# Context layers of 16 heads: second-half maxima moved into the batch's own attention, maxima spread among projections, shift chain apart

## The chip, the core and the metric

The kernel runs on one NeuronCore of a Trainium2 chip. A core has a matrix engine (TensorE, PE in the profile, with its weight loads listed apart as PEld), a vector engine (DVE), an activation engine (ACT), a general engine (POOL) and a queue that issues transfers (SP). [...] The metric is the device time of one execution in microseconds (us), lower is better.

## The reference, cut to what matters

The program is a chain of attention layers over `x` of 4 batches, 1024 tokens and 256 channels. The context `ctx` has 77 tokens a batch. Everything is float32.

```python
# layer "sa"+"ca": pre-norm self-attention (16 heads, masked), cross-attention to ctx (16 heads of 16), feed-forward 256 -> 1024 -> 256
h = layernorm(x, ln1);  x = x + mha(h, h, h, sa, mask)
h = layernorm(x, ln2);  x = x + mha(h, ctx, ctx, ca)
h = layernorm(x, ln3);  x = x + relu(h @ w1 + b1) @ w2 + b2
# three layers of 4 heads of 64: the first attends to ctx, two to themselves
for i in range(3): x = layer4(x, ctx if i == 0 else x)
# "l2" and "l3": cross-attention to ctx, 16 heads of 16, residual, post-norm ("l2" has an output projection)
for layer in (l2, l3):
    scores = einsum(q, k) / scale          # per batch: 16 x 1024 x 77
    attn = softmax(scores)
    x = layernorm(attn @ v [@ wo] + x)
return x
```

The softmax subtracts each row's maximum before the exponential. In this kernel that maximum is found by computing the scores a first time with tokens on the partitions ("maxima"), and is then added into the scores of the attention proper, which have keys on the partitions, by a small matmul ("shift").

## The kernel before

**Items and units.** `Net.rest` lines up 28 items: layers `sa` (class `SelfFew`), `ca` (`Cross16`), three layers of 4 heads (`Cross4`, then `Self4` twice), `l2` and `l3` (`Cross16` both), each for batches 0 to 3. In this text "l2 1" is layer l2 on batch 1. `Pipe.run` goes through the items one after the other. An item's attention is a row of units; a `Cross16` item has 8: four groups of four heads (g = 0..3) for the first half of the tokens (c = 0), then four for the second half (c = 1). TensorE's program order is exactly the order in which the Python code emits (`manual_schedule`); the order on the other engines is left to a scheduler, which can put a ready instruction ahead of one emitted earlier.

**One unit** (`Pipe.unit`) emits the scores of a group (line 346, eight matmul records, and line 352, the four matmuls that add the shift), then calls the pump, then emits the finishing transposes of the group before (line 377), and last the weighted sum (line 365) of its own group, which waits for the two exponentials on ACT (line 356).

**The pump** (class `Pump`) puts other work into the units. It has two lists of steps, each with a cost, perhaps a test that must hold and a lag that should pass after it. The first list holds the steps of the next item's `start` (and, for `Self4`, `more` of the item itself); the second holds the steps of the item before's `end`. At unit n of N it takes steps until the done share of all costs reaches n/N, choosing, among list heads whose test holds and whose lag is over, the one of the list that is less far; the last unit takes all that is left, lags or not. If no head is due, the unit ends early. `Pump.until` takes steps of the first list until a test holds: attention on half c asks that `c + 1` halves are prepared.

**The steps of `Cross16.start`** prepare an item while the item before it attends: `new` (tiles; POOL computes the spread keys `ka`; DVE the statistics where a norm comes first), and for each half `norm`, two `turn`s (transposes to channels, line 252), two `query` projections (line 260), eight `maxima` (line 270: two pairs of matmul records each, into two of the four one-bank PSUM tiles `p1`; line 275: two reductions on DVE), `shift`, `have_half`. `shift` first splits the maxima into three bfloat16 parts by four short DVE instructions (lines 304 to 307) and then transposes them on TensorE (line 310) and copies them out, alternately on DVE and ACT (`evac`).

**The steps of `end`** finish the item before: `turn` and `project` (lines 412 and 419; not in l3, which has `plain`), `stats` (lines 1483, 1484) and `norm` (lines 1530, 1533) for l2 and l3, with a reciprocal root on POOL between them; for `ca` the feed-forward (`Feed.steps`, lines 562 to 600), whose matmuls are 16 `hidden` and 8 `out` steps. The normalized tile `xn` (tag "F") has one buffer, shared by `Cross16`, `SelfFew` and `Feed`.

Of the kernel before, what the change touches and what calls it, by code (L numbers as in the profile page):

```python
# [17 lines left out]
P = 128  # L18
# [65 lines left out]
class Pump:  # L84
# [31 lines left out]

    def until(self, test):
        while not test():
            self.take(0)


class Pipe:
# [26 lines left out]
    def run(self, items):  # L149
        pump = Pump(self, 1, items[0].start(), [])  # L150
        pump.until(lambda: items[0].halves >= 1)
        left = pump.lists[0]
        before = None
        for a, b in zip(items, items[1:]):
            b.prev = a
        for i, item in enumerate(items):
            last = i + 1 == len(items)
            first = left + ([] if last else items[i + 1].start())
            second = (before.end() if before else []) + (item.end() if last else [])
            left = []  # L160
            idle = item.idle()
            self.pump = pump = Pump(self, item.units + idle, item.more() + first, second)
            for _ in range(idle):
                self.unit()
            for scores in item.attend():
                self.unit(scores, item.cost)
            before = item
        while self.due:
            pump.n = 0
            self.unit()  # L170
        pump.n = pump.units - 1
        pump()


class Item:
# [4 lines left out]

    def more(self):

        return []

    def idle(self):

# [2 lines left out]
    def __init__(self, net, layer, b):  # L189
        self.net, self.l, self.b = net, layer, b  # L190
        self.halves, self.ended = 0, 0
        self.prev, self.later_half = None, True

    def room(self):

# [9 lines left out]
class Cross16(Item):  # L205
# [7 lines left out]
    def start(self):  # L213

        net, l, b, h = self.net, self.l, self.b, H16
        nc, work, x = net.nc, net.work, net.x[b]
        steps = l.steps() if b == 0 else Steps()
        step = steps.add

        def new():  # L220
            self.hT = net.tile("C", [P, NC, S], name="hT")
            self.sh = net.tile("SH", [P, 2, 512], BF16, name="SH")
            self.mx = net.small.tile([P, NT, h.n], F32, tag="mx", name="mx", bufs=2)
            self.ka = net.work.tile([P, 2, 4, SC], F32, tag="KA", name="KA", bufs=2)
            for e in range(2):
                nc.gpsimd.tensor_tensor(
                    self.ka[:, e, :, :], l.kt[:, e, ts(b, SC)].unsqueeze(1).to_broadcast([P, 4, SC]),
                    net.own4.unsqueeze(2).to_broadcast([P, 4, SC]), ALU.mult,
                )
            if l.norm is not None:  # L230
                self.mv = net.moments(b)
                self.rstd = net.rsqrt_var(self.mv, 1e-5)

        def new_q():
            self.qt = net.tile("A", [P, 2, S], name="QT")

        def norm(c):
            if l.norm is None:
                self.xn = x[:, 4 * c : 4 * c + 4, :]
                return  # L240
            mv, rstd = self.mv, self.rstd
            self.xn = net.tile("F", [P, 4, C], name="xn")
            for i in range(4):
                t = 4 * c + i
                nc.vector.tensor_scalar(
                    self.xn[:, i, :], x[:, t, :], mv[:, t, 0:1], rstd[:, t : t + 1], ALU.subtract, ALU.mult
                )

        def turn(c, cc):
            pt = net.p1.tile([P, 512], F32, tag="p1", name="pt")  # L250
            for i in range(4):
                nc.tensor.transpose(pt[:, ts(i, P)], self.xn[:, i, ts(cc, P)], net.ident)
            at = None if l.norm is None else COL_LN + 4 * (l.norm - 1) + cc
            g, be = (None, None) if at is None else (net.cols[:, at : at + 1], net.cols[:, at + 2 : at + 3])
            net.evac(self.hT[:, cc, ts(c, 512)], pt, g, be)

        def query(e, c):
            pp = net.p1.tile([P, 512], F32, tag="p1", name="pp")
            for cc in range(NC):
                nc.tensor.matmul(  # L260
                    pp, l.w["wq"][:, cc, ts(e, P)], self.hT[:, cc, ts(c, 512)], start=cc == 0, stop=cc == NC - 1
                )
            nc.scalar.activation(self.qt[:, e, ts(c, 512)], pp, AF.Identity, bias=net.bias16[:, l.at + e : l.at + e + 1])

        def maxima(e, t):

            pas = [net.p1.tile([P, 4, SC], F32, tag="p1", name="pa") for _ in range(2)]
            for i in range(2):
                rows = slice(64 * i, 64 * i + 64)
                nc.tensor.matmul(  # L270
                    pas[i], self.qt[rows, e, ts(t, P)], self.ka[rows, e, :, :], start=True, stop=True
                )
            for i in range(2):
                out = self.mx[:, t, :].rearrange("p (j g) -> p j g", j=4)[:, 2 * i : 2 * i + 2, 2 * e : 2 * e + 2]
                nc.vector.tensor_reduce(  # L275
                    out, pas[i].rearrange("p (j s) k -> p j s k", s=2), AX.X, ALU.max, negate=True
                )

        ln = l.norm is not None
        step(0, new, lag=8 * ln)  # L280
        for c in range(2):
            step(0, norm, c, lag=3 * ln)
            step(0.5, turn, c, 0)
            step(0.5, turn, c, 1, lag=2)
            if c == 0:
                step(0, new_q, test=self.room)
            for e in range(2):
                step(1.8, query, e, c)
            for e in range(2):
                for i in range(4):  # L290
                    step(0.55, maxima, e, 4 * c + i, lag=3 if (e, i) == (1, 3) else 0)
            step(0.3, self.shift, c)
            step(0, self.have_half)
        return steps

    def shift(self, c):

        net, h = self.net, H16
        nc = net.nc
        m = self.mx[:, 4 * c : 4 * c + 4, :].rearrange("p t (j g) -> p t j g", j=4)  # L300
        m3, rest = net.m3[c], net.rest16[c]
        parts = [m3.rearrange("p t (j r) -> p t j r", j=4)[:, :, :, i : 3 * G : 3] for i in range(3)]
        left = rest.rearrange("p t (j g) -> p t j g", j=4)
        nc.vector.tensor_copy(parts[0], m)
        nc.vector.tensor_tensor(left, m, parts[0], ALU.subtract)
        nc.vector.tensor_copy(parts[1], left)
        nc.vector.tensor_tensor(parts[2], left, parts[1], ALU.subtract)
        pm = net.p1.tile([P, 512], BF16, tag="p1", name="pm")
        for i in range(4):
            nc.tensor.transpose(pm[:, ts(i, P)], m3[:, i, :], net.identb)  # L310
        net.evac(self.sh[:, c, :], pm)

    def shift_by_row(self, c):
# [217 lines left out]
class Feed:  # L531
# [15 lines left out]
    def steps(self, b):  # L547
        net, nc, x = self.net, self.net.nc, self.net.x[b]
        s = {}
        steps = Steps()  # L550
# [6 lines left out]

        def norm(c):
            s["xn"] = net.tile("F", [P, 4, C], name="xn")
            for i in range(4):  # L560
                t = 4 * c + i
                nc.vector.tensor_scalar(
# [3 lines left out]
        def turn(c, cc):  # L566
# [2 lines left out]
                nc.tensor.transpose(pt[:, ts(i, P)], s["xn"][:, i, ts(cc, P)], net.ident)  # L569
            at = COL_LN + 8 + cc  # L570
            net.evac(s["hT"][:, cc, ts(c, 512)], pt, net.cols[:, at : at + 1], net.cols[:, at + 2 : at + 3])

        def hidden(q, f):

# [28 lines left out]
            step(0, self.load)  # L603
        step(0, new, lag=8)
        for c in range(2):
            step(0, norm, c, lag=3)
            step(0.5, turn, c, 0)
            step(0.5, turn, c, 1, lag=2 * c)
        for q in range(4):
# [24 lines left out]
class Self16(Cross16):  # L634
# [8 lines left out]
    def start(self):  # L643
# [18 lines left out]

        def norm(c):
            self.xn = net.tile("F", [P, 4, C], name="xn")
            net.normal(self.xn, x, self.mv, self.rstd, c)

        def turn(c, cc):
            net.turn_normal(self.hT, self.xn, 1, c, cc)

        def query(g, c):  # L670
            pp = net.p1.tile([P, 512], F32, tag="p1", name="pp")
# [49 lines left out]
        step(0, new, lag=8 if b else 0)  # L721
        for c in self.cs:
            if b:
                step(0, norm, c, lag=3)
                step(0.5, turn, c, 0)
                step(0.5, turn, c, 1, lag=2)
            step(1.8, query, 0, c)
# [100 lines left out]
class SelfFew(Cross16):  # L828
# [5 lines left out]
    def start(self):  # L834
# [21 lines left out]

        def norm(c):
            self.xn = net.tile("F", [P, 4, C], name="xn")
            net.normal(self.xn, x, self.mv, self.rstd, c)

        def turn(c, cc):
            net.turn_normal(self.hT, self.xn, 1, c, cc)

        def query(e, c):
            pp = net.p1.tile([P, 512], F32, tag="p1", name="pp")
# [57 lines left out]
        step(0, new, lag=8 if b else 0)  # L923
        for c in self.cs:
            if b:
                step(0, norm, c, lag=3)
                step(0.5, turn, c, 0)
                step(0.5, turn, c, 1, lag=2)
            if c == 1:
# [3 lines left out]
            if c == 1:  # L933
                step(0.9, values)
            for t in range(4 * c, 4 * c + 4):
                step(0.9, maxima, t, lag=3 if t % 4 == 3 else 0)
            step(0.3, self.shift, c)
            step(0, self.have_half)
        return steps
# [495 lines left out]
class Net:  # L1435
    def __init__(self, ctx, tc, t):
        self.ctx, self.tc, self.nc, self.t = ctx, tc, tc.nc, t
        self.flip = 0

    def evac(self, out, src, scale=None, bias=None):

# [694 lines left out]
```

## Time and profile before

| | |
|---|---|
| time, median of 3 runs (lowest to highest) | 2431.14 us (2427.19 to 2433.52) |
| the profiled execution's own time | 2428.16 us |
| its span, first to last instruction | 2426.3 us |
| TensorE busy, matmul / weight load | 91% / 51% of the span |
| VectorE, ScalarE, GpSimd busy | 67%, 37%, 4% |
| mean granted TensorE clock | 0.944 |
| maxima: line 270 matmul / line 275 reductions | 768 records, 170.9 us / 384 reductions, 157.6 us |
| plain 16-head context units: line 346 / line 356 | 112.7 us / 185.4 us |

How to read what follows: the windows view lists, for a stretch given in us from the span's start, each engine's busy time, then the TensorE clock that was granted (1.00 is full speed), then the transfers' share. The timeline lists groups of like instructions: start, length, engine, line, operation, destination and sources, count, and in brackets the idle time of that engine just before and what ended it.

### The profile page before, as it was taken

The page shows a single profiled execution, that of the slowest core. Times are in us where ns is not written, and L with a number is a line of the kernel's source. Part 1 is how long each engine was busy: PE and PEld are TensorE (multiplying, and loading weights), DVE is VectorE, ACT ScalarE, POOL GpSimd, SP SyncE. Part 2 cuts the span into 40 slices and gives each one's busy share as a digit, 9 for nine tenths or more (in the row PEclk, how much of TensorE's full clock was granted, in tenths as well). Part 3 has the DMA queues.
Part 4 walks back from the last instruction along what each step waited for, and adds up shares of the span by engine and source line. Part 5 has one row for each costly group of instructions (what it writes and reads, how often), then busy time and mean ns, then how long its engine had stood idle before and what let it go on. Part 6 is the DMA issues. An engine that isn't in the chain of part 4 may idle for free. (4 is left out here: it accounts for less than half of the span.)

```text
span 2426.3 us, 29759 instructions
## 1 busy us (share of the span) xinstructions
PE 2201.2 (91%) x11003; PEld 1233.3 (51%) x11003; DVE 1620.2 (67%) x3200; ACT 907.2 (37%) x1700; POOL 104.2 (4%) x142
## 2 busy tenths in 40 slices
PE   4899999999999989999998999999998898899886
PEld 2566546666768655544444544444444444454332
DVE  5566655444243777888888788888888655565665
ACT  1222342222331544444444445444433343334333
POOL 2000000000000000000000000000000000000000
PEclk7999999999989989999999999989999898899888
DMA  4000010000000001766665666666675300000000
GB/s 127 18 1 16 5 35 1 1 7 5 7 5 3 1 5 45 157 150 139 139 144 134 146 148 148 139 139 139 156 160 130 70 5 1 5 1 1 27 18 28
DMA packets 197593, 158.18 MB, mean 65 GB/s; under 512 B 51327, under 2 KB 196030, under 8 KB 197438
## 3 DMA queue, kind: packets, MB, share of 16 engines
q1 hardware_dynamic: 195374, 152.45, 27.3%
q0 software_dynamic: 1008, 2.68, 0.5%
q8 instruction: 90, 1.47, 0.3%
q10 hardware_dynamic: 1056, 1.05, 0.1%
q14 instruction: 65, 0.53, 0.1%
HBM read 17.67 MB, written 4.19 MB: 9 GB/s over the span
## 5 line engine op out<-in xcount | busy, mean ns | idle before, releaser
L1230 ACT ACTIVATE PR<-ss,nm 128x1024 f32<-128x1024 f32 x256 | 284.4, 1113 | 398.9 <-DVE nm L1224 313.1
L1242 DVE STREAM_TRANSPOSE PR<-PR 128x2048 f32<-128x2048 f32 x128 | 295.8, 2311 | 113.4 <-ACT PR L1230 109.9
L1213 PE MATMUL ss<-QK 64*128 64x512 f32 x1024 | 336.9, 650 | 38.1 <-ACT PR L1230 37.8
L1224 DVE TENSOR_REDUCE nm<-ss 128x1 f32<-128x1024 f32 x256 | 299.8, 1210 | 9.5 <-PE ss L1213 9.4
L1285 PE MATMUL po<-PT,V 128*64 128x256 f32 x2048 | 261.3, 399 | 9.0 <-DMA PT<-PR 6.8
L356 ACT ACTIVATE PT<-pb 77x1024 f32<-77x1024 f32 x192 | 185.4, 1016 | 173.7 <-PE pb L352 173.7
L1285 PEld LDWEIGHTS po<-PT,V 128*64 128x64 f32 x2048 | 141.7, 141 | 171.6 <-issue 109.2
L1213 PEld LDWEIGHTS ss<-QK 64*128 64x128 f32 x1024 | 116.7, 193 | 181.9 <-ACT PR L1230 105.7
L275 DVE TENSOR_REDUCE mx<-pa 128x4 f32<-128x308 f32 x384 | 157.6, 469 | 74.2 <-PE pa L270 73.1
L270 PE MATMUL pa<-KA,QT 64*128 64x308 f32 x768 | 170.9, 499 | 33.7 <-DVE mx L275 31.1
L270 PEld LDWEIGHTS pa<-KA,QT 64*128 64x128 f32 x768 | 103.4, 201 | 101.9 <-DVE mx L275 46.8
L365 PE MATMUL po<-PT,Vc 77*32 77x512 f32 x768 | 135.7, 646 | 18.9 <-ACT PT L356 10.2
L1452 ACT COPY OT<-po 128x512 f32<-128x512 f32 x57 | 33.4, 586 | 230.1 <-PE po L365 218.4
L595 PE MATMUL pp<-w,hid 128*128 128x256 f32 x512 | 114.0, 381 | 0.0
L580 PE MATMUL pp<-hF,w 128*128 128x256 f32 x512 | 113.2, 379 | 0.0
L346 PE MATMUL pb<-QT,KA 32*77 32x512 f32 x768 | 112.7, 658 | 0.0
L595 PEld LDWEIGHTS pp<-w,hid 128*128 128x128 f32 x512 | 96.5, 190 | 15.9 <-DVE mx L275 2.5
L580 PEld LDWEIGHTS pp<-hF,w 128*128 128x128 f32 x512 | 97.1, 190 | 14.6 <-issue 1.3
L1483 DVE BATCH_NORM_STATS2 st<-x 128x6 f32<-128x256 f32 x256 | 97.9, 404 | 5.6 <-DMA x<-in_x 4.4
L1356 PE MATMUL pp<-wo,hE 128*128 128x256 f32 x384 | 96.4, 393 | 1.6 <-ACT hE L1459 1.5
L588 ACT ACTIVATE hid<-pp,cols 128x256 f32<-128x256 f32 x64 | 30.4, 474 | 175.7 <-PE pp L580 175.7
L260 PE MATMUL pp<-hT,wq 128*128 128x512 f32 x192 | 91.2, 611 | 1.8 <-DVE hT L1450 1.0
(253 smaller groups left out, 3042.3 us busy)
## 6 DMA issues: line engine op xcount, KB each, us to landing
PT<-PR SPq DMA_DIRECT2D x1024, 128.0 KB
x<-in_x SPq DMA_DIRECT2D x4, 1024.0 KB
out<-x SPq DMA_DIRECT2D x8, 512.0 KB
w<-in_ff_w SPq DMA_DIRECT2D x2, 1024.0 KB
gb<-in_norms POOLq DMA_DIRECT2D x5, 256.0 KB, 4.8
wk<-in_l_wk SPq DMA_DIRECT2D x10, 128.0 KB
wv<-in_l_wv SPq DMA_DIRECT2D x5, 256.0 KB
wq<-in_l_wq SPq DMA_DIRECT2D x10, 128.0 KB
```

Source lines behind the costliest of these rows:

```text
L270: nc.tensor.matmul(pas[i], self.qt[rows, e, ts(t, P)], self.ka[rows, e, :, :], start=True, stop=True)
L275: nc.vector.tensor_reduce(out, pas[i].rearrange("p (j s) k -> p j s k", s=2), AX.X, ALU.max, negate=True)
L346: nc.tensor.matmul(pbs[j // 2][:SC, j % 2, :], self.ka[rows, e, 2 * (j % 2) + s, :], self.qt[rows, e, ts(c, 512)], start=True, stop=False,)
L356: nc.scalar.activation(pt[:, 2 * i : 2 * i + 2, :], pbs[i][:SC], AF.Exp, scale=self.l.scale)
L365: nc.tensor.matmul(po[ts(j, h.slot), :], l.v[:, self.b, col : col + h.vw], pt[:, j, :], start=True, stop=True)
L580: nc.tensor.matmul(pp[:, i, :], self.w1[:, cc, ts(f + i, P)], s["hT"][:, cc, ts(q, 2 * P)], start=cc == 0, stop=cc == NC - 1)
L595: nc.tensor.matmul(pp[:, u, :], s["a"][:, f, ts(u, P)], self.w2[:, f, :], start=f == 0, stop=f == NF - 1)
L1213: nc.tensor.matmul(ss[h][:, k, :], self.qk[p][rows, 0, ts(t, P)], self.qk[p][rows, 1, ts(k, 512)], start=True, stop=True,)
L1224: nc.vector.tensor_reduce(self.nm[:, t, at], s2, AX.X, ALU.max, negate=True)
L1230: nc.scalar.activation(out, s2, AF.Exp, bias=self.nm[:, t, at], accum_out=self.sums[:, t, at])
L1242: nc.vector.transpose(part, part)
L1285: nc.tensor.matmul(po[64 * h : 64 * h + 64], self.v[:, k, 64 * (2 * p + h) : 64 * (2 * p + h) + 64], pts[:, :, h, :, k, :] if net.blocks e ...
```

## The change

- The second half's eight `maxima`, its split and its `shift` leave `start` and become `rest`, which `more` hands to the pump at the head of the first list when the item's own attention begins.
- In `start`, both halves are normalized and turned before any maxima; the two `query` steps of the second half are put after the first four maxima of the first half and after its split. Every maxima step has a lag of 0.5.
- The split of the maxima (`thirds`) becomes a step of its own, ahead of the transposes (`shift`), with a lag of 2 or 3.
- A flag `held` is set by `norm` when it takes the one `xn` tile and cleared by the second `turn`; another `norm` has the test `not_held`. `until` takes from the second list where the first list's head fails its test.
- No instruction is added or removed; the arithmetic is the same.

```diff
     def until(self, test):
         while not test():
-            self.take(0)
+            first = self.lists[0][0]
+            self.take(0 if first.test is None or first.test() or not self.lists[1] else 1)
...
+            assert last or not any(pump.lists)
             before = item
...
     def more(self):

-        return []
+        return self.rest
...
             self.xn = net.tile("F", [P, 4, C], name="xn")
+            net.held = True
...
             net.evac(self.hT[:, cc, ts(c, 512)], pt, g, be)
+            if cc and at is not None:
+                net.held = False
...
         step(0, new, lag=8 * ln)
-        for c in range(2):
-            step(0, norm, c, lag=3 * ln)
+        def turns(c):
+            step(0, norm, c, lag=3 * ln, test=net.not_held if ln else None)
             step(0.5, turn, c, 0)
             step(0.5, turn, c, 1, lag=2)
-            if c == 0:
-                step(0, new_q, test=self.room)
-            for e in range(2):
-                step(1.8, query, e, c)
+
+        turns(0)
+        step(0, new_q, test=self.room)
+        for e in range(2):
+            step(1.8, query, e, 0)
+        turns(1)
+        self.rest = Steps()
+        for c in range(2):
+            step = (steps, self.rest)[c].add
             for e in range(2):
                 for i in range(4):
-                    step(0.55, maxima, e, 4 * c + i, lag=3 if (e, i) == (1, 3) else 0)
+                    step(0.55, maxima, e, 4 * c + i, lag=0.5)
+                if c == 0 and e == 0:
+                    step(1.8, query, 0, 1)
+            step(0, self.thirds, c, lag=2)
+            if c == 0:
+                step(1.8, query, 1, 1)
             step(0.3, self.shift, c)
             step(0, self.have_half)
         return steps

-    def shift(self, c):
-
-        net, h = self.net, H16
+    def thirds(self, c):
+
+        net = self.net
         nc = net.nc
...
         nc.vector.tensor_tensor(parts[2], left, parts[1], ALU.subtract)
+
+    def shift(self, c):
+
+        net = self.net
+        nc = net.nc
         pm = net.p1.tile([P, 512], BF16, tag="p1", name="pm")
         for i in range(4):
-            nc.tensor.transpose(pm[:, ts(i, P)], m3[:, i, :], net.identb)
+            nc.tensor.transpose(pm[:, ts(i, P)], net.m3[c][:, i, :], net.identb)
         net.evac(self.sh[:, c, :], pm)
...
             for t in range(4 * c, 4 * c + 4):
-                step(0.9, maxima, t, lag=3 if t % 4 == 3 else 0)
+                step(0.9, maxima, t)
+            step(0, self.thirds, c, lag=3)
             step(0.3, self.shift, c)
```

The last lines are those of `SelfFew`. `Feed`, `SelfFew` and `Self16` (which this data does not run) set and clear `held` in the same way, and their `norm` steps get the test `not_held`.

## The prediction

> **What bounds the kernel now.** I read the page (TensorE 91% busy, clock 0.944), the waits, then the 16-head units in the windows view, and the timeline where they run long. First, whole stretches: the last two units of `sa` 3, `ca` 0, `ca` 1, `ca` 3, the end of `Self4`, `l2` 0 to 3, `l3` 0, `l3` 1 and `l3` 3. Read the length and the clock, third value from the end.
>
> ```profile
> 246.06:276.09 30.03, 25.24 (x117) 15.41 (x115) 24.37 (x67) 5.90 (x8) 3.19 (x3) 1.00 0.00 1
> 276.09:336.75 60.66, 56.58 (x349) 29.15 (x349) 33.14 (x82) 24.07 (x30) 1.36 (x2) 1.00 0.02 5
> 336.75:456.33 119.58, 116.69 (x620) 79.61 (x616) 55.77 (x147) 33.69 (x49) 5.50 (x4) 1.00 0.06 18
> 576.37:687.87 111.50, 107.52 (x578) 76.25 (x574) 37.00 (x93) 36.76 (x56) 3.86 (x7) 0.98 0.02 7
> 1882.30:1916.41 34.11, 27.22 (x129) 16.18 (x128) 22.34 (x36) 7.43 (x16) 0.00 (x0) 0.75 0.54 124
> 1916.41:1980.78 64.37, 61.99 (x374) 30.98 (x373) 40.03 (x110) 26.03 (x35) 4.19 (x5) 1.00 0.02 5
> 1980.78:2047.70 66.92, 58.20 (x349) 29.18 (x345) 41.52 (x107) 24.22 (x31) 3.83 (x4) 0.92 0.00 1
> 2047.70:2116.58 68.88, 61.13 (x349) 31.51 (x345) 39.59 (x105) 24.54 (x31) 2.22 (x2) 0.87 0.04 5
> 2116.58:2186.06 69.48, 63.68 (x372) 34.75 (x368) 39.46 (x105) 25.41 (x33) 5.16 (x6) 0.92 0.00 1
> 2186.06:2258.93 72.87, 60.72 (x348) 30.50 (x344) 43.58 (x119) 24.32 (x31) 4.74 (x5) 0.87 0.02 8
> 2258.93:2317.02 58.09, 51.83 (x301) 21.93 (x297) 35.95 (x99) 21.97 (x27) 3.58 (x4) 0.88 0.06 19
> 2375.08:2426.30 51.22, 32.56 (x200) 9.43 (x196) 26.88 (x76) 18.38 (x21) 3.33 (x3) 0.87 0.10 33
> ```
>
> Single units of l3: one with three maxima, a plain one, the one after a split of the maxima, and one with two turns beside a norm.
>
> ```profile
> 2277.65:2282.93 5.28, 5.23 (x41) 2.21 (x37) 3.87 (x12) 1.93 (x2) 0.00 (x0) 1.00 0.01 3
> 2384.87:2389.24 4.37, 3.80 (x27) 1.07 (x25) 3.16 (x9) 2.52 (x3) 0.19 (x1) 1.00 0.14 47
> 2317.02:2322.50 5.48, 5.48 (x36) 2.50 (x32) 1.81 (x4) 2.99 (x4) 0.00 (x0) 0.71 0.00 0
> 2345.38:2353.87 8.49, 4.83 (x38) 2.07 (x37) 6.59 (x21) 2.89 (x4) 1.11 (x1) 0.83 0.00 0
> ```
>
> The timeline: three maxima in a row and their shift; then one lone maxima step up to the next PE instruction.
>
> ```profile
> 2309.35 2.52 PE L270 MATMUL pa<-KA,QT 64*128 64x308 f32 x12
> ...
> 2310.17 2.40 DVE L275 TENSOR_REDUCE mx<-pa 128x4 f32<-128x308 f32 x6 [2.24 <-PE pa L270]
> ...
> 2313.76 0.61 PE L310 MATMUL pm<-identb,m 128*128 128x128 bf16 x4 [1.89 <-DVE m L307]
> ```
> ```profile
> 2269.29 0.79 PE L270 MATMUL pa<-KA,QT 64*128 64x308 f32 x4
> ...
> 2270.01 0.66 PE L377 MATMUL pt<-ident,OT 128*128 128x128 f32 x4
> ```
>
> TensorE's order sets the end: it is busy nearly throughout, and what it loses is seen here. Each split costs it a wait of 1.89 us. In each l2 batch it also waits 2.4 to 5.0 us, in the fourth and the eighth unit, for reductions that stand on DVE behind `stats` and `norm`. And after such waits the clock is halved: the share is (1 - 0.79)·2 of the 8.92 us from 2308.10 and (1 - 0.71)·2 of the next 5.48, together 6.9 us after one split, so up to 3.4 us lost.
>
> **Prices, in us.** A plain unit takes 4.34 (4.37 and 4.31 in turn); 1.5 of it is waiting for the exponentials, which other work can fill (4.34 + 2.45 - 5.28). So a unit costs the larger of 4.34 and 2.85 + its work. A lone maxima step takes 0.72 (2269.29 to 2270.01), three in a row 2.45, and each further one 0.8, which is DVE's pace (2.40 for six reductions). `query` 1.82 and `project` 1.81 (3.63 and 3.62 for two), a `turn` 0.52 (1.04 for two), the transposes of `shift` 0.33. From the last maxima to them 1.96 pass (4.41 less 2.45).
>
> **The new order.** I stepped the pump's two lists by the costs in the code; for the kernel before that gives the order that the trace shows. The result:
> - l2 1, l2 2, l3 0, units 1 to 4: three maxima and two turns; two maxima and two projects; one maxima; one maxima. Then, forced by `until`, one maxima, split and shift with nothing between them. Units 5 to 8: two turns; two queries and four turns; three maxima and two projects; one maxima, a query, four maxima, split, query, shift.
> - l3 1 to 3: one maxima in each of units 1 to 4, the other four in the forced group.
> - `ca` 1 to 3: maxima beside `turn` and `project`; forced groups of three, three and two; then three plain units, whose work has gone to unit 8, to the feed-forward.
>
> A forced group adds a wait: TensorE stands at line 310 for the split, behind it stand the next unit's scores, and behind those ACT's exponentials.
>
> **Part by part**, each against its stretch above.
>
> 1. `sa` 3's last unit loses eight maxima (6.4), a split's wait and shift (2.3), and the remaining split goes under a query (1.8): -10.4. `ca` 0 takes eight maxima and gives eight away: -0.7.
>
> 2. `ca` 1: units 5.33 + 7.19 + 4.61 + 7.19, group 2.45 + 1.96 + 0.33, three plain ones 13.0, the last 70.4 + 6.8 of moved turns and queries + 1.6 where a `norm` (four 0.36 instructions on DVE) waits for the one `xn` tile with no matmul left above it: 120.9, so +1.3. `ca` 2 (120.04 before) +0.9. `ca` 3 takes over the share that `sa` 3 gave up, less the 5 us that it now loses in its fourth unit: +7.4. The three groups may lower the clock; bounds 0 and 3.4 each, I take 1, since TensorE is busy on both sides of them: +3. With part 1: +1.5.
>
> 3. End of `Self4`: eight maxima and a shift leave, 8.7 of TensorE time. Bounds 8.7 and 17 (half of the 34.11 ran at half clock, so half of that can return besides); I add only the wait of 3.46 that ends at 1891.30: -12. `l2` 0 takes the eight: its units add up to 64.7 by the prices, with 3.5 of waits on `Self4`'s statistics and 2.5 for the clock 70.7, against 64.4: +6.3.
>
> 4. l2 1, l2 2, l3 0: 6.05 + 7.91 + 4.34 + 4.34, group 3.2 (0.82 to the first reduction, 0.86 for two, 1.19 for the split, 0.33), 4.34 + 8.57 + 8.63 + 10.88 (2.85 + 0.72 + 1.82 + 3.2 + 1.96 + 0.33) = 58.3. Per half, DVE still has 7.1 of `stats` and `norm`, and how long the reductions stand behind them the trace can't show: bounds 0 and 3.7 a half (the excess of 2345.38 over 4.34, less its clock). I take 3.5 for both halves, nearer to none, since a query now runs ahead of the four maxima, and 3 for the clock: 64.8. Three times that is 194.3, against 208.7: -14.4.
>
> 5. l2 3: units 36.7 and a last one of 28.6 with all of l3 0's keys, values, turns and queries = 65.3, waits and clock 4.5: 69.8, +0.3. What SP and POOL issue is the same: l3's weights and POOL's two 0.70 products for `ka` come some four units later and still precede their use by units; the feed-forward weights, issued at 347.6, are used at 391.5, and a later issue by a few us leaves more than 20. Covers that fail here would cost their delay.
>
> 6. l3 1 and l3 2: 17.4 for four units in which the maxima cost nothing, group 5.5 (3.2 + 1.96 + 0.33), 4.34 + 7.53 + 4.34 + 12.6 = 51.7; waits 1.5, clock 2.4: 55.6 against 58.1, -2.5 each. l3 3 gets eight maxima that it didn't have: four are free, the group costs 5.5, the clock 1.1 (5.48 less 4.37), and its first unit regains 1.1: +5.5. Together +0.5.
>
> The sum is 1.5 - 12 + 6.3 - 14.4 + 0.3 + 0.5 = -17.8. The profiled execution took 2428.16 us (span 2426.3), so 2410.4; the median stood 3.0 above it: **2413 us**.
>
> A plain unit, with its two short waits, runs at clock 1.00 (2384.87), and so the plain units left in `ca` are in the sum at 4.34. [...]
>
> **Rivals.** *The groups stall* (slower). In the seven groups of l2 0, 1, 2 and l3 0 to 3 the last reductions and the split wait on DVE behind `norm`, with no matmul above them. For it: in the unit of 2345.38 TensorE loses 3.7 because a copy stands behind `norm` on DVE; with 3.4 for half clock 7.1 a group, where some 2.5 are allowed: +32, 2445 us. It decides from 2.5 more a group (17.8 / 7). Against it: these reductions are emitted ahead of the `norm` they would wait for. *The waits only move* (no change). In l2's last units five reduction pairs, `stats` and `norm` still share DVE, and the query gives no cover: part 4 is 0, 2427 us. For it: DVE's work in an item is the same. Against it: the stretch from 1941.17 to 1955.15, where two queries precede eight maxima beside a norm, waits only 0.9. *It doesn't spread the maxima* is partly true, by the forced groups and the last units, and is in the sum.
>
> **Chances.** The forecast 0.56, no change 0.18, stalled groups 0.26. About 0.3% (7 us) is what a measurement of this kernel can tell from no change, so these are also the chances of faster, same and slower. The range goes down to 2396 (part 3 at its bound, -5; l2 without waits and with half the clock loss, -12) and up to 2441, most of the way to the stalled groups.
>
> **What would show it.** Right: the wait at line 310 leaves the last units of l2 and l3 and appears before their fifth; the end of `Self4` is 10 us shorter at a higher clock; l2 batches take 63 to 67; l3 3 is some 5 longer. Wrong: l2 batches of 67 or more, waits of TensorE for line 275 above the 22.9 us that l2 and l3 have now, or plain units of `ca` below clock 1.00.

## The result, and the profile after

The changed kernel takes 2422.63 us (median of 18 runs, 2413.55 to 2431.47) beside 2433.86 us of the kernel before in the same comparison. The ratio is 0.9956, with a 95% interval of 0.9943 to 0.9969: faster by 0.44%, or 11.2 us between the medians, and the interval lies wholly below 1. The profiled execution took 2416.46 us, its span is 2414.7 us (2426.3 before), its mean granted clock 0.954 (0.944 before).

The windows view of the changed kernel, stretch by stretch (length first, granted clock third from the end): the last unit of `sa` 3, `ca` 2, `ca` 3, the second half of the last `Self4` item, `l2` 0, `l2` 2, `l3` 3. Behind them stands that half of `Self4` in the kernel before.

```profile
244.03:265.86 21.83, 21.26 (x88) 11.34 (x86) 17.02 (x42) 5.32 (x7) 1.36 (x2) 1.00 0.00 1
452.24:582.27 130.03, 123.20 (x620) 79.25 (x616) 58.05 (x150) 33.88 (x49) 4.26 (x4) 0.93 0.02 4
582.27:707.36 125.09, 117.88 (x613) 78.43 (x609) 44.58 (x114) 36.97 (x56) 3.87 (x7) 0.97 0.03 6
1845.53:1923.34 77.81, 70.81 (x354) 35.30 (x353) 58.91 (x78) 27.74 (x53) 0.00 (x0) 0.95 0.59 136
1923.34:1991.70 68.36, 63.72 (x378) 31.65 (x376) 41.42 (x110) 27.02 (x37) 4.19 (x5) 0.93 0.07 12
2055.47:2115.97 60.50, 57.49 (x348) 27.38 (x344) 39.13 (x105) 24.50 (x31) 2.21 (x2) 0.97 0.01 1
2354.26:2414.67 60.41, 41.91 (x236) 14.19 (x232) 34.77 (x97) 18.38 (x21) 3.33 (x3) 0.79 0.09 28
```
```profile
1824.61:1916.41 91.80, 82.81 (x392) 45.91 (x392) 68.36 (x98) 30.05 (x57) 0.00 (x0) 0.87 0.54 121
```

`ca` 2 and `ca` 3 (120.04 and 111.50 before) are longer at a lower clock, the unit of `sa` 3 (32.18) is shorter, the half of `Self4` (91.80) shorter at a higher clock, `l2` 2 shorter at a higher clock, `l3` 3 longer at a lower one. The stretches that the prediction priced, in us, between the two profiled executions:

| Part | Predicted | Measured |
|---|---|---|
| 1: up to the end of `ca` 0 | -11.1 | -9.8 |
| 2: `ca` 1 to `ca` 3, clock included | +12.6 | **+29.3** |
| 3: last `Self4` item and `l2` 0 | -5.7 | -7.4 |
| 4: `l2` 1, `l2` 2, `l3` 0 | -14.4 | -18.7 |
| 5: `l2` 3 | +0.3 | -2.0 |
| 6: `l3` 1 and 2 / `l3` 3 | -5.0 / +5.5 | -11.1 / +9.2 |
| layers of 4 heads in between | 0 | -1.2 |
| sum | -17.8 | -11.6 |

TensorE's waits in l2 and l3, before and then after (us in all, times, longest):

```profile
PE pa L270 <- DVE mx L275: 22.9, 8, 5.0
PE pm L310 <- DVE m L307: 13.2, 6, 3.7
```
```profile
PE pa L276 <- DVE mx L281: 10.4, 8, 2.6
PE pm L331 <- DVE m L323: 15.1, 9, 2.1
```

The waits for the reductions (line 275, now 281) are halved. Those for the split (line 307, now 323) are as long as before: they left the last units and came back in the forced groups, where TensorE now stands 1.3 to 2.1 us before each fifth unit of l2 and l3.

A second count goes through what follows. The trace records the granted clock in steps of 3.413 us, each at full or at half speed. Half of TensorE's busy time inside halved steps is what the clock can have cost (an estimate from the trace, and an upper bound: a plain unit of `ca` 2, the one from 488.49 shown below, stood at half clock throughout and took 6.30 us for 4.31, where half of its busy time is 3.1). It is 111.3 us before and 94.4 after. So by this count the clock gave 16.9 us where the spans differ by 11.6, and the rest took 5.3 back. From `l2` 1 to `l3` 2 the count falls from 38.1 to 10.7, which is 27.4 of the 31.7 us that these items gain; in `ca` 1 to 3 it rises from 3.4 to 13.4.

### The profile page after: what moved, and what is told of

The parts are those of the page before. It is cut to its first block, busy times and chain, and to the rows that moved or that the text cites. A ratio compares the mean times of both kernels' runs of the same rounds, so it can differ in the third digit from the quotient of the medians.

```text
span 2414.7 us, 29718 instructions
## 1 busy us (share of the span) xinstructions
PE 2207.1 (91%) x11003; PEld 1205.9 (50%) x11003; DVE 1620.6 (67%) x3200; ACT 908.2 (38%) x1700; POOL 103.0 (4%) x142
## 3 DMA queue, kind: packets, MB, share of 16 engines
q1 hardware_dynamic: 195374, 152.45, 27.4%
## 5 line engine op out<-in xcount | busy, mean ns | idle before, releaser
L276 PE MATMUL pa<-KA,QT 64*128 64x308 f32 x768 | 166.9, 482 | 13.0 <-DVE mx L281 11.4
L276 PEld LDWEIGHTS pa<-KA,QT 64*128 64x128 f32 x768 | 83.1, 191 | 95.3 <-issue 32.2
L604 PE MATMUL pp<-hF,w 128*128 128x256 f32 x512 | 118.6, 386 | 0.0
L604 PEld LDWEIGHTS pp<-hF,w 128*128 128x128 f32 x512 | 96.8, 192 | 18.7 <-issue 6.0
L440 PE MATMUL pp<-wo,aT 128*128 128x256 f32 x384 | 90.8, 386 | 0.0
```

What stands on the lines that cost most here:

```text
L276: nc.tensor.matmul(pas[i], self.qt[rows, e, ts(t, P)], self.ka[rows, e, :, :], start=True, stop=True)
L604: nc.tensor.matmul(pp[:, i, :], self.w1[:, cc, ts(f + i, P)], s["hT"][:, cc, ts(q, 2 * P)], start=cc == 0, stop=cc == NC - 1)
```

## The experiments

My theory after the result: the gain comes from moving the second half out of the last units, where it shares DVE with statistics and norm, and the loss from the forced groups. The rivals: it comes from the split as a step apart, from the order and the lags inside the halves, or from windows of half clock that fall by chance. Ratios are to the kernel before, with their 95% interval.

### The parts of the change by layer

`e2_not_in_ca` and `e3_only_in_ca` choose by layer between the two orders (`e2_not_in_ca`, and the kernels below that have ca in the old order, also take the test `not_held` from the `norm` of `Feed` again):

```diff
         ln = l.norm is not None
+        if ln:            # e3: if not ln
+            ...           # the steps of the kernel before, then return
         step(0, new, lag=8 * ln)
```

> The changed kernel, with the steps of layer ca in the order of the kernel before (l2 and l3 as changed). Measured so far, in one profile each: from the start to the first unit of ca 10.2 us less, ca 0 to ca 3 together 29.7 us more. My theory (the parts add up, and what the change does in ca is a loss): 19.5 us less than the changed kernel, about 2403 (ratio to before 0.9875), with every item of l2 and l3 within 1 us of the changed kernel. The rival (the differences are windows of half clock that fall by chance, since the stretches start elsewhere): l2 and l3 differ by several us an item although their order is the same, and the total stays within 8 us of the changed kernel, 2415 to 2430.

> The other half: the changed order in layer ca alone, l2 and l3 as in the kernel before. My theory: 19.5 us more than before, about 2453 (ratio 1.008); the end of Self4, l2 and l3 within 1 us an item of the kernel before. The rival of chance windows: within 8 us of the kernel before.

Without ca: 2403.36 us, ratio 0.9873 (0.9854 to 0.9892). Only ca: 2458.72 us, 1.0099 (1.0079 to 1.0119). The first meets the theory, the second is 6 us slower than the 2453 that I expected. By the ratios the change is worth 31 us in l2 and l3 and costs some 24 in ca, and the two add up to the whole within about 5 us. Item for item l2 0 to l2 3 of the first stand within 0.4 us of the changed kernel. But the rival of chance has a share: `l2` 2 of the second takes 3.6 us more than in the kernel before, in the same order. `l3` 3 runs the same instructions in 60.41, 63.99 and 56.30 us in three kernels, and `ca` 2 in 130.03, 132.75 and 133.02.

### The split apart

```diff
-                    step(0.55, maxima, e, 4 * c + i, lag=3 if (e, i) == (1, 3) else 0)
+                    step(0.55, maxima, e, 4 * c + i)
+            step(0, self.thirds, c, lag=3)
             step(0.3, self.shift, c)
```

> The kernel before with one part of the change alone: the split of the maxima is a step of its own, with the lag behind it, in Cross16 and in SelfFew; every maxima step stays where it was. My theory (the gain is from where the second half's maxima and the forced groups stand): the scheduler already puts the split on DVE right behind the last reduction, and in the last units nothing stands between split and shift, so the time stays within 3 us of the kernel before. The rival (the split as a step apart is what pays): 5 us or more faster than before.

1.0025 (1.0005 to 1.0045): no gain, rather 0.25% lost, which is 6 us and twice what I allowed; the interval goes from 1 to 11 us. In its profile the stretch from the first layer of 4 heads to `l2` 0, whose order is the same, is 7 us longer, while l2 and l3 together are 3 us shorter. The split apart alone doesn't pay.

### l2 0 prepared in Self4 again

```diff
+        if isinstance(self.prev, Self4):
+            ...           # the steps of the kernel before, then return
```

> The changed kernel, but l2 0 prepares both its halves in Self4 as in the kernel before, so that sixteen of its maxima stand in the last item of Self4 again; l2 1 to l3 3 as changed. My theory (eight maxima are dear at the end of Self4, where TensorE ran at half clock, and cheap in l2 0): the end of Self4 takes 11 us more again, l2 0 about 5 less, so some 6 us more than the changed kernel, 2428. The rival (the waits only move: what Self4 saves l2 0 pays): within 2 us of the changed kernel.

2421.89 us, 0.9947 (0.9925 to 0.997): not told apart from the changed kernel's 0.9956, so the rival holds. The last half of `Self4` takes 92.49 again, and `l2` 0 only 54.23, together 146.72; in the changed kernel they take 77.81 + 68.36 = 146.17. What `Self4` saves, `l2` 0 pays. The move is a relay: each item hands eight maxima on, the first one (`sa` 3, `Self4`) gets shorter and the last one (`ca` 3, `l3` 3) longer.

### Matmuls under the wait of the groups

```diff
+        if c == 1 and type(self) is Cross16:
+            pd = net.p1.tile([P, 512], F32, tag="p1", name="pd")
+            for k in range(2 if self.l.norm is None else 3):
+                nc.tensor.matmul(pd, net.ident, self.qt[:, k % 2, ts(1, 512)], start=True, stop=True)
         pm = net.p1.tile([P, 512], BF16, tag="p1", name="pm")
```

> The changed kernel, with matmuls put under the wait of the forced groups: ahead of the second half's shift transposes TensorE runs two more 128x512 matmuls (three in layer ca), whose result nobody reads, in a tile of p1. They add work, some 1.8 us a group (2.7 in ca), where TensorE stood idle for 1.3 to 2.9. My theory: in the trace the clock is granted in steps of 3.41 us; after a step at full clock in which TensorE was busy under 40% the next is always halved, and from half clock it returns only after a step that was busy 80% or more, so plain units, which wait in each, stay halved once they are. So with the group's wait covered the plain units behind it run at clock 1.00, 4.3 to 4.4 each, and the unit behind each group of l2 loses its excess: the losses at half clock behind the groups, summed in the profile of the changed kernel, are 20 us, so 15 to 20 us less than the changed kernel's median, 2403 to 2408. [...]

Of the three units behind the group of `ca` 2 in the windows view, the first two in the changed kernel, and then the last two with the cover:

```profile
483.23:488.49 5.26, 5.12 (x26) 1.54 (x24) 3.47 (x16) 2.52 (x3) 1.80 (x2) 0.61 0.00 0
488.49:494.79 6.30, 6.25 (x27) 1.65 (x25) 2.89 (x7) 1.93 (x2) 0.00 (x0) 0.50 0.00 0
```
```profile
495.63:500.38 4.75, 2.90 (x26) 0.93 (x25) 3.76 (x10) 1.93 (x2) 0.00 (x0) 1.00 0.02 3
500.38:504.77 4.39, 3.79 (x28) 1.07 (x24) 0.68 (x2) 2.52 (x3) 0.00 (x0) 1.00 0.00 0
```

Clock 1.00, and so in all nine plain units behind the groups but the last two of `ca` 1: in these seven the half clock came from the group's wait, and not from the short waits of the plain units. But the time is 2420.72 us, 0.9957 (0.9944 to 0.9971), as without the cover; my 15 to 20 us did not come. By stretches `ca` 2 and 3, `l2` 1 and 2, `l3` 1 and 3 took 16.2 us less. `ca` 0, whose shift never waited, took 2.7 more for its three matmuls, `ca` 1 5.3 more (half clock from its sixth unit on, where a wait of 1.85 for a copy stands), `l3` 2 3.6, the first layer of 4 heads 2.3. Whether the last two are chance the runs don't settle.

### Maxima in threes

```diff
-                    step(0.55, maxima, e, 4 * c + i, lag=0.5)
+                    step(0.55, maxima, e, 4 * c + i, lag=0.5 if c == 0 or 4 * e + i in (2, 5, 7) else 0)
```

> The kernel with ca in the old order, and the second half's maxima without lag inside threes (three, three, two), so that several go into one unit and the split is emitted a unit ahead of its shift; until then forces the shift alone (l3 3 still has a forced group of three, since its list is short). My theory: no wait for the split is left in l2 0 to l3 2, nor the half clock behind it: by the prices l2 1, l2 2, l3 0 save 3 us each, l3 1 and l3 2 4 each, l2 0 4, l2 3 and l3 3 1 each, 23 in all, against 2403: 2380. The rival (the waits only move: the maxima bunched in threes wait for DVE at line 276 instead): within 5 us of 2403.

2425.45 us, 0.9969 (0.9953 to 0.9985): 22 us slower than 2403, beyond my theory and its rival. Its waits in l2 and l3:

```profile
PE pa L276 <- DVE mx L281: 18.2, 9, 4.1
PE pt L415 <- DVE mx L281: 9.5, 3, 3.2
...
PE pm L348 <- DVE m L340: 2.9, 3, 1.9
```

The split's waits are gone, as planned, from 15 to 2.9. In their place stand 27.7 us for the reductions of the threes (10.1 in the kernel without threes), in units that hold `stats` or `norm` of DVE too.

### The move undone, the rest kept

```diff
-            step = (steps, self.rest)[c].add
+            step = steps.add
```

> The kernel with ca in the old order, and in l2 and l3 one part of the change undone: the second half's maxima, split and shift stay at the end of start, in the item before; the turns ahead of the maxima, the queries between them, the lags and the split as a step apart stay as changed. My theory (what pays is that the second half leaves the last unit of the item before, where statistics and norm share DVE with it): the last units of l2 0 to l3 2 hold eight or more maxima in a row, the gain of l2 and l3 is gone, 25 us or more above 2403, 2428 or more. The rival (the queries between the maxima and the split under a query are what pays): half of the gain or more stays, 2418 or less.

2401.19 us, 0.9877 (0.9858 to 0.9897). My theory falls: without the move the kernel is as fast as with it in l2 and l3 (2403). Its `l2` 2 in the windows, units 4 and 8, beside units 3 and 4 of the kernel before:

```profile
2066.16:2070.47 4.31, 4.31 (x33) 1.37 (x29) 3.32 (x11) 1.93 (x2) 1.11 (x1) 1.00 0.00 0
...
2083.51:2110.66 27.15, 23.76 (x114) 13.52 (x112) 19.63 (x55) 5.04 (x7) 1.01 (x1) 0.91 0.11 11
```
```profile
2063.30:2070.12 6.82, 6.77 (x48) 3.36 (x44) 3.86 (x11) 2.52 (x3) 0.00 (x0) 1.00 0.00 0
2070.12:2081.75 11.63, 8.80 (x49) 4.70 (x45) 9.35 (x28) 1.93 (x2) 1.11 (x1) 0.71 0.00 0
```

Units 4 to 7 carry one maxima each and last no longer than a plain one (4.31 to 4.37). Before, three and five stood in a row, TensorE waited 2.83 us in the second of these units, and the clock fell to 0.71.

The last unit (27.15 us) does hold eight maxima in a row beside the `norm`, as I had said, and yet TensorE waits only 0.83 us there for reductions. The timeline shows where `norm` stands: in unit 4 before, its four instructions of line 1533 are ahead of the reductions, while here they stand singly between them. The wait of unit 4 before, with what it waits behind, and then the one of the last unit here:

```profile
2073.39 1.67 DVE L1533 SCALAR_TENSOR_TENSOR x<-x,pw,gb 128x256 f32<-128x256 f32 x4 [0.90 <-POOL pw L1492]
...
2075.50 3.83 PE L270 MATMUL pa<-KA,QT 64*128 64x308 f32 x12 [2.83 <-DVE mx L275]
```
```profile
2099.43 5.43 PE L276 MATMUL pa<-KA,QT 64*128 64x308 f32 x22 [0.83 <-DVE mx L281]
```

### Lag or order: a square of four

The lag alone, in the kernel before (`e8_lag_alone`), and the order without the lag (`e11_order_alone`, from `e7_not_moved`):

```diff
-                    step(0.55, maxima, e, 4 * c + i, lag=3 if (e, i) == (1, 3) else 0)
+                    step(0.55, maxima, e, 4 * c + i, lag=3 if (e, i) == (1, 3) else 0 if ln else 0.5)
```
```diff
-                    step(0.55, maxima, e, 4 * c + i, lag=0.5)
+                    step(0.55, maxima, e, 4 * c + i)
```

> The kernel before with one small part of the change alone: in l2 and l3 every maxima step has a lag of 0.5 instead of none (3 stays on the last); order, queries, turns, shift and ca are as before. My theory now, after the kernel without the move was as fast as with it (2401 against 2403): what pays is that maxima no longer come in bursts of three to five, for which TensorE waits 2.4 to 5 us on DVE and then runs at half clock, but one to a unit, under the wait for the exponentials; so two thirds or more of the 30 us of that kernel come from the lag alone: 2405 to 2412, with the last units of l2 and l3 long (25 us or more) and no clock lost in the units before them. The rival (the queries between the maxima and the early turns are what pays, as cover in the last units): within 5 us of before, 2427 or more.

> The kernel with ca in the old order and nothing moved (2401), with one thing undone: the maxima of l2 and l3 have no lag, so the pump takes them in rows again; turns first, queries between the maxima and the split apart stay. With the lag alone (2410) it makes a square of four kernels. My theory (the lag pays 21 of the 30 us, the order 9): the order alone brings some 9 us against before, 2419 to 2427. The rival (each of the two takes away the same waits, so either brings most of it): 2412 or less.

Lag alone 2409.61 us, 0.9913 (0.9884 to 0.9942), in the range of my theory; order alone 2408.46 us, 0.9909 (0.9885 to 0.9932), in that of its rival. So either brings some 21 to 24 us, and both together 30. My sign for the lag, last units of 25 us or more, holds in two of seven only (20.2 to 30.0 us). Their waits in l2 and l3, the lag first:

```profile
PE pm L310 <- DVE m L307: 23.3, 10, 3.8
...
PE pa L270 <- DVE mx L275: 3.9, 7, 0.9
```
```profile
PE pa L276 <- DVE mx L281: 14.3, 7, 4.1
...
PE pm L348 <- DVE m L340: 5.7, 3, 1.9
```

The lag takes away the waits for the reductions (22.9 to 3.9) and makes those for the split longer (13.2 to 23.3), the order takes away most of the split's (5.7) and some of the reductions' (14.3). The order is three things at once: early turns, queries between the maxima, and the split apart. The last alone gave nothing; the first two were not run one without the other.

### Nothing moved, in ca either

The same edit as in `e7_not_moved`, made in the changed kernel itself, so that ca keeps the new order of turns, queries and lags.

> The changed kernel less the move alone: rest is empty in all layers, so the second half's maxima, split and shift stay in start, also in ca; turns, queries, lags and the split apart as changed, also in ca. My theory (in ca it is the move that costs: the forced groups, and the lag of the next item's new, which then comes late and leaves three plain units without work): ca takes what it took before, within 4 us over its four items, and the total is 2398 to 2406. The rival (the new order inside the halves is what costs in ca): ca 0 to ca 3 stay 15 us or more above before, 2415 or more.

2410.23 us, 0.9908 (0.9888 to 0.9927), above my 2398 to 2406 and below the rival's 2415. `ca` 0 to 3 take 419.3 us, 7.5 above before (411.8): the order costs that much, mostly a wait of 4.1 for a split at the end of `ca` 1 and `ca` 2. Against the changed kernel's 0.9956 the move itself is a loss of some 12 us; since it made no difference in l2 and l3 (2403 and 2401), this loss is that of ca.

### Moved in l2 alone, and covered

```diff
-            step = (steps, self.rest)[c].add
+            step = (steps, self.rest if l.has_wo else steps)[c].add
```

> ca in the old order, the second half moved into the own attention in l2 alone, and in l3 left in the item before. By the two kernels that had it everywhere in l2 and l3 and nowhere: with the time that TensorE lost to half clock taken out, the end of Self4 with l2 0 to l2 2 is 13 us shorter with the move, l2 3 to l3 3 some 7 us shorter without it. So if the parts add up: 2403 less 7 to 10, 2393 to 2397, the best of all. The rival (both halves of that sum are chance windows of half clock): 2401 to 2405, no better than either.

2397.89 us, 0.9861 (0.9838 to 0.9884). That is 1 us above my range, and not told apart from 0.9873 and 0.9877 by the intervals. On top of it the cover, two matmuls in l2 and l3:

> The best kernel so far (moved in l2 alone, ca in the old order, 2398) with two unread 128x512 matmuls ahead of the second half's shift in l2 and l3, where TensorE otherwise waits 1.3 to 3.2 us for the split. My theory (the wait is there anyway, and a wait that fills most of one 3.41 us step halves the clock of the next): the matmuls cost nothing, 0.5 in l2 3, and the 10 to 15 us that this kernel's profile loses to half clock from the end of Self4 to l3 3 shrink by half or more: 2388 to 2393. The rival (covering one wait lets the next one halve the clock, as when the groups of the changed kernel were covered and the time stayed): within 4 us of 2398.

2390.34 us, 0.9823 (0.9804 to 0.9843), within my range, and all five runs (2381.06 to 2395.2) below all four without the cover (2396.84 to 2399.04): the fastest kernel here, 1.8% under the kernel before. Measured against the kernel before, the two intervals still touch (0.9838 to 0.9843), so the cover's own gain, 7.5 us between the medians, is likely and not shown beyond doubt. TensorE's wait for the split in l2 and l3 without the cover, and then the waits left with it:

```profile
PE pm L348 <- DVE m L340: 16.2, 8, 3.2
```
```profile
PE pa L276 <- DVE mx L281: 5.9, 6, 2.0
...
PE pm L352 <- DVE m L340: 1.6, 3, 1.3
```

In these two profiles, which lie 15.8 us apart, the mean granted clock is 0.957 and 0.964, and what the clock can have cost falls from 86.2 us to 67.4. In l2 and l3 it falls from 16.9 to 3.8, and the items take 479.6 us for 490.3; the other 5.6 of the count lie in stretches whose instructions are the same, so chance has a part in them. That the cover works here, because few other waits are left that could halve the clock in its stead, fits these figures and was not tested by itself.

## Why the prediction was right, and where it was wrong

The direction and the range hold: 2422.63 against 2413, inside 2396 to 2441, a gain of 11.2 us where I had 17.8. The order that I stepped from the costs is the order that ran. Most of what was named as a sign of right is there: the split's wait before the fifth units, a last half of `Self4` that is 14.0 shorter at a higher clock, reductions' waits below 22.9 (10.4). Signs of wrong are there too: the plain units of `ca` 1 to 3 below clock 1.00, `l2` 0 and `l2` 3 above 67 (68.36 and 67.51, which the prices themselves had at 70.7 and 69.8), and `l3` 3 longer by 9.2 instead of 5. That the total came so near is partly luck: part 2 cost 16.7 us more than I had, `l2` 1 to `l3` 2 gained 12.6 more. Four steps failed or were mis-sized.

- **Part 2 is the one that cost the sum: +29.3 for +12.6.** Of the 16.7 missing, 4.0 are the nine plain units, which took 46.1 us for 39.1 with 3 allowed for the clock. My statement that they run at clock 1.00 holds where they are entered at full clock (`ca` 0: 4.37, 4.31, 4.37), and fails behind a group, as the cover showed. The groups took 2.5 more: between the reductions and the split DVE also does statistics of other batches, which the scheduler had put there, so that TensorE waited 2.91 in `ca` 1, where I had 1.96 from the last maxima to the transposes.

```profile
356.34 0.22 DVE L321 TENSOR_TENSOR rest<-mx,m 128x64 f32<-128x64 f32 x1
356.48 0.42 DVE L1518 BATCH_NORM_STATS2 st<-x 128x6 f32<-128x256 f32 x1
356.82 0.22 DVE L322 CAST m<-rest 128x64 bf16<-128x64 f32 x1
```

  The timeline shows two of the split's four instructions with a statistics instruction of another batch between them. The first three units took 2.7 more (0.9 an item), and the last ones 7.5, of which 1.7 in `ca` 1 and 1.6 in `ca` 2 is a query that waits for the copy of the turn right ahead of it; the rest of that is not taken apart. By the second count the clock alone can have cost 10.0 more in `ca` 1 to 3 than before, where I had allowed 3.
- **Parts 4 and 6 were too small, and for the wrong reason.** l2 1 to l3 2 gain 31.7 where I had 19.1. I put the gain on the move. The runs put it on the lag, which lets maxima stand one to a unit, and on the order, with queries between the maxima and the split: the same 30 us come without the move. The price behind it was right (a maxima step in a plain unit is free), I only credited it to the wrong edit. By size, l2 1, l2 2 and l3 0 were priced at 64.8 each and took 63.77, 60.50 and 65.72; l3 1 and l3 2 at 55.6, and took 53.01 and 52.05, because the 3.9 that I allowed there for waits and clock mostly didn't come.
- **Part 3** met its number (the last `Self4` item -11.4 for -12, `l2` 0 +4.0 for +6.3), but it isn't a gain of the change: with `l2` 0 prepared in `Self4` again the time is the same.
- **`l3` 3** had 1.1 for the clock and lost 4.1 of its 9.2 to it, in this profile: its three plain units take 5.39, 6.29 and 5.48 us, and 4.37, 4.31 and 4.36 with the group covered. The same group cost nothing in `l3` 2.

Of the rivals, *the groups stall* named the right spot in the wrong layer: in l2 and l3 the groups themselves cost what I gave them (7.5 to 7.7 us for the fourth units of `l2` 1, `l2` 2 and `l3` 0, where I had 4.34 + 3.2), in ca more. *The waits only move* is true of the split's waits (13.2 to 15.1) and not of the reductions'. The plain units do lose the clock (0.61, 0.50 and 0.70 in `ca` 2), in seven of nine through the wait ahead of them. That their own short waits then keep it down, as I wrote ahead of the cover, is not shown: the four half steps from 484.44 on, in which those of `ca` 2 stand, were 96 to 100% busy.

## What to carry to other kernels

Ask of a gain which edit it needs: spreading maxima steps one to a unit, under a wait that is there anyway, or the new order with independent matmuls between a burst and its dependent step, gave 21 to 24 us each, while the move that gave the change its name cost 12, all of it in ca. A step that is moved into the next item is paid there, and the last of the chain pays for all. An idle time on TensorE can cost more than its length: in `l3` 3 a wait of 1.89 us was followed by 4.1 us lost to half clock. Where nothing useful can fill it, even unread matmuls may: under all the groups of the changed kernel they left the time as it was (2420.72 for 2422.63), and in l2 and l3 alone, with few other waits left, the median was 7.5 us lower, a gain that is likely and not beyond doubt.

## What the runs showed of the hardware

The granted clock goes by steps of 3.413 us in these traces, and a wait costs by where it falls in them. The groups of `l3` 1, 2 and 3 in the changed kernel are the same, each with a wait of 1.89 us. By steps of the trace (windows of 3.41 us, clock third from the end), the step of the wait and the next one in `l3` 1, then both steps that share the wait in `l3` 2:

```profile
2269.61:2273.02 3.41, 1.52 (x13) 0.82 (x15) 2.64 (x9) 0.14 (x1) 0.00 (x0) 1.00 0.00 0
2273.02:2276.44 3.42, 3.42 (x19) 1.73 (x12) 0.35 (x1) 1.80 (x3) 0.00 (x0) 0.50 0.00 0
2320.81:2324.22 3.41, 2.75 (x14) 1.67 (x12) 3.41 (x9) 0.00 (x0) 0.00 (x0) 1.00 0.02 5
2324.22:2327.64 3.42, 2.19 (x22) 1.30 (x23) 1.04 (x5) 1.05 (x2) 0.00 (x0) 1.00 0.01 2
```

In `l3` 1 the wait falls into one step, busy for 1.52 of 3.41 us, and the next is halved. In `l3` 2 it is shared between two (2.75 and 2.19 busy) and nothing follows. In the profiles of the kernel before and of the changed one together, a step at full clock that was busy under 40% was followed by a half one in 29 cases of 29, at 40 to 70% in 39 of 82, at 70 to 80% in 2 of 62, above that in 0 of 1089. After a half step that was busy under 80% full clock came back in 0 cases of 36, and above that in 68 of 106. The steps don't begin at the same point of the two spans: the first half one begins at 23.02 us before and at 23.64 after. So the same instructions can differ by several us an item from kernel to kernel: `l3` 3 took 60.41, 63.99 and 56.30 us, and of the first, in the changed kernel, up to 6.8 us are the clock's by the second count.
